# A Perceiver block with routed experts on one core: second-layer biases at the evacuation, first queries among the first scores, rotary tables as a step of their own, first expert weights sooner

## The chip, the core and the metric

The kernel runs on one core of a Trainium2 chip. The engines are TensorE (PE, its weight loads shown as PEld), VectorE (DVE), ScalarE (ACT), GpSimd (POOL) and SyncE (SP); each works through its own queue of instructions and waits on semaphores of the others. SP computes nothing here and issues most of the DMAs. All data are float32. The time is that of one execution on the device, in microseconds (us), and the median of several runs is compared. The kernel before took 834.33 us (median of 3 runs, 834.09 to 838.12).

## The reference

Input x has 64 sequences of 32 tokens with 256 channels (2048 tokens); each sequence has a context of 257 rows of 128 channels.

```python
x = x + xattn(layernorm(x), ctx)      # 16 heads of 64, no mask
x = x + attn(layernorm(x))            # 4 heads of 64, half of each head rotated by position
x = x + ffn(layernorm(x))

# attn: tables from one learned number
base = sigmoid(nrope_freq[0]) * SDT_L + MIN_L * BASE_FREQUENCY
inv_freq = base ** (-arange(16) / 16)
ang = pos[:, None] * inv_freq[None, :] * (2 * pi / (T - 1))     # cos(ang), sin(ang)

# ffn: 8 experts, 2 a token, gates renormalised over the two
scores = x @ Wr.T + br
h = x @ Wl1[n] + bl1[n]; a, b = split(h)
y[n] = (silu(a) * b) @ Wl2[n] + bl2[n]
out = sum over the two chosen n of gate[n] * y[n]
```

## The kernel before

Tokens are cut into 16 tiles of 128 (t = 0 to 15), each four sequences (b = 0 to 3). The program has three stages: a start, an attention loop over the 64 sequences, and an expert stage.

The queues of PE and SP keep the order in which the program is written; a planner orders the instructions of DVE, ACT and POOL, within their dependencies, before the program is compiled.

**Start.** `load` (L98) puts a DMA on SP's queue: the rotary base number `base` (L129), the first two tiles of x, the query weights `xwq_sb` and `xwk_sb` (1 MB and 0.5 MB, one DMA each, L132 and L133), the first context, then the other weights. POOL fills constants: `diag`, `u_ring` and `p_last` (L166 on) with zeros, and a row of iotas. `cross_queries(0)` (L305) normalises two tiles of x (`normed`: statistics on DVE, the inverse root as a power on POOL, the product on DVE), transposes them on PE, copies them on ACT to `xqT`, and makes the queries of 16 heads in four groups: `pqh` (PE, L345), its copy `qh` (ACT), `pq` (PE, L324, folding the key weights into the query), and its copy `q` by halves on DVE (L337) and ACT (L335). The rotary tables `cos` and `sin` are computed next in the text (L890 to L928): a sigmoid on ACT, a power of 16 elements on POOL (L913), two sines on ACT (L919, L920), doubled twice on DVE. After that the rest of `cross_queries(0)`, and `cross_probs` of the first sequence.

**Attention loop** (L935). For each sequence: `tp` transposes its probabilities (PE, L392), `s` makes scores of the next sequence in four groups (PE, L369), each with its negative maximum `nmx` (DVE, L373), exponential (ACT, L374), reciprocal of the sums and product `pr` (DVE, L379, L381), and `pa` mixes the context (PE, L402). Between these `step()` advances one of three generators by a unit, as the table `steps` (L875) says: six places for each of eight sequences, two tiles. "ahead" makes queries of the tiles to come. "near" is `rest` of the tile just finished and "far" that of the tile before it; `rest` runs `cross_output` (`pov`, `po`), `self_attention` (`trs`, `pqkv`, the rotation on DVE, `trqk`, `pss`, `pot`, `apo`) and `route` (L526). `route` ends with the expert choice (`trr`, `pr`), the slots (`pk`, L567, L568), two indirect DMAs by POOL which scatter the token rows and their gates into the DRAM table `routed` (L578), and the bias path: the eight gates of a token are transposed (`pw`, PE, L586), copied (DVE, L588), multiplied with the eight second-layer biases `b2` (`pb`, PE, L591), added to x (DVE, L592), and x is written to `out` (L595).

PSUM tiles called `bank` share three banks, in turn.

**Expert stage.** A block is 128 rows of `routed` of one expert. Six early blocks are formed from the tiles counted so far when t = 15 begins (`early_blocks`, L771), and 33 late ones at most after the last tile (`late_blocks`, L800, a long chain on DVE from the counts `pc_late` to the addresses `meta_late`). A block has the units x (`prepared`: rows transposed, gate and target row taken), a and b (first layer, by halves), c (`combined`: second layer `py`, its product with the gate by DVE, L762, and an indirect DMA of POOL that adds the rows to `out`, L763). Weights lie in three lanes of SBUF, the first layer in one tile (`wall1`) and the second in another (`wall2`, 4 KB a partition); a load is skipped when the expert stays the same. The end of the attention work and the early blocks are woven by a list of units written by hand (L1015 to L1025).

The early rows are fetched in the last tile (L974 to L977):

```python
        if t == NT - 1 and b == 2:
            load_last(t)
            for i in range(EARLY):
                blocks.gathered(i)
            blocks.weights(0, (0, 1), sure=True)
```

The tile `xg` that a gather fills has five buffers, and `EARLY` is 6.

Of the kernel before, what the change touches and what calls it, by code (L numbers as in the profile page):

```python
# [16 lines left out]
P = 128  # L17
# [18 lines left out]
W2LEN = 4 * D  # L36
# [14 lines left out]
def block_kernel(  # L51
# [21 lines left out]
    b2: bass.AP,  # L73
# [17 lines left out]
    half_pi = const.tile([P, 1], FP, name="half_pi")  # L91
    nc.gpsimd.memset(half_pi, math.pi / 2)
# [36 lines left out]
    load(base, freq.partition_broadcast(P))  # L129
    for t in range(2):  # L130
        load_tokens(t)
    load(xwq_sb, xwq.rearrange("(c p) k -> p c k", p=P))  # L132
    load(xwk_sb, xwk_t.rearrange("(c p) k -> p c k", p=P))  # L133
# [15 lines left out]
    b2_sb = const.tile([NE, D], FP, name="b2_sb")  # L149
# [7 lines left out]
    load(b2_sb, b2)  # L157
# [6 lines left out]

    diag = [const.tile([P, AH, P], FP, name=f"diag{i}") for i in range(2)]
    for d in diag:  # L166
        nc.gpsimd.memset(d, 0.0)

    u_ring = [const.tile([P, D], FP, name=f"u{i}") for i in range(3)]
    p_last = [
        [const.tile([P, 32], FP, name=f"p_last{i}_{b}") for b in range(4)] for i in range(2)
    ]
    for u in u_ring:
        nc.gpsimd.memset(u, 0.0)
    for ring in p_last:
        for p in ring:
            nc.gpsimd.memset(p, 0.0)

    def iota(shape, pattern, base, by_partition, name):
        it = const.tile([P] + shape, FP, name=name)
        nc.gpsimd.iota(
            it,
            pattern,
            base=base,
            channel_multiplier=by_partition,
            allow_small_or_imprecise_dtypes=True,
        )
        return it  # L190

    ones = const.tile([P, P], FP, name="ones")
    nc.gpsimd.memset(ones, 1.0)

    before = iota([P], [[1, P]], 0, -1, "before")
    nc.vector.tensor_scalar(before, before, 0.0, None, ALU.is_gt)
    region = iota([1, NE], [[0, 1], [CAP, NE]], 0, 0, "region")
    expert_id2 = iota([2, NE], [[0, 2], [1, NE]], 0, 0, "expert_id2")

    upto = iota([NE, NE], [[1, NE], [-1, NE]], 0, 0, "upto")  # L200
    nc.vector.tensor_scalar(upto, upto, 0.0, None, ALU.is_ge)

    late = iota([LATE], [[1, LATE]], 0, 0, "late")
    in_lane = iota([LATE // LANES, LANES], [[1, LATE // LANES], [0, LANES]], FAR, 0, "in_lane")
    late_expert = iota([LATE, NE], [[0, LATE], [1, NE]], 0, 0, "late_expert")

    early = iota([EARLY // 2, 2], [[1, EARLY // 2], [EARLY // 2, 2]], 0, 0, "early")
    early_expert = iota([EARLY, NE], [[0, EARLY], [1, NE]], 0, 0, "early_expert")
    row = iota([1], [[0, 1]], 0, 1, "row")
    minus_spare = iota([1], [[0, 1]], -TOK, -1, "minus_spare")  # L210
    token = iota([NT], [[P, NT]], 0, 1, "token")

    seen = const.tile([P, NE], FP, name="seen")
    nc.gpsimd.memset(seen, 0.0)
    xp = pool("xp", 3)
    none = xp.tile([P, RW], FP, tag="xg", bufs=5, name="none")
    nc.gpsimd.memset(none, 0.0)

    for e in range(NE):
        load(routed[e * CAP : e * CAP + P, :], none)  # L220

    load(out[TOK : TOK + P, :], none[:, :D])

# [4 lines left out]
    sm = pool("sm", 4)  # L228
    tb = pool("tb", 1)
# [4 lines left out]
    def normed(t, name, xn=None):  # L234
        st = sm.tile([P, 6], FP, tag="st", name=f"st{name}{t}")
        mv = sm.tile([P, 2], FP, tag="mv", name=f"mv{name}{t}")
        nc.vector.bn_stats(st, xs[t])
# [67 lines left out]
    def cross_queries(c):  # L305

        xqT = wk.tile([P, 2, 2 * P], FP, tag="xqT", name=f"xqT{c}")
        xns = [normed(2 * c + j, "q") for j in range(2)]
# [133 lines left out]
    def self_attention(t, xn):  # L442
# [4 lines left out]
        for lo, hi in ((0, 512), (512, 768)):  # L447
            pq = bank([hi - lo], f"pqkv{t}_{lo}")
            for k in range(2):
                nc.tensor.matmul(  # L450
                    pq, xaT[:, k, :], awqkv_sb[:, k, lo:hi], start=(k == 0), stop=(k == 1)
                )
            nc.vector.tensor_tensor(qkv[:, lo:hi], pq, abqkv_bc[:, lo:hi], ALU.add)

# [5 lines left out]
        nc.vector.tensor_tensor(x1s, x1, sb, ALU.mult)  # L460
# [64 lines left out]

    def route(t, xr):  # L526

# [56 lines left out]
        yield  # L584
        pw = bank([P], f"pw{t}")
        nc.tensor.transpose(pw[:NE, :], ew, ident)  # L586
        ewT = sm.tile([NE, P], FP, tag="rewT", bufs=2, name=f"rewT{t}")
        nc.vector.tensor_copy(ewT, pw[:NE, :])  # L588
        yield
        pb = bank([D], f"pb{t}")  # L590
        nc.tensor.matmul(pb, ewT, b2_sb, start=True, stop=True)  # L591
        nc.vector.tensor_tensor(xs[t], pb, xs[t], ALU.add)  # L592

        queue = nc.sync if t < NT - 2 else nc.gpsimd
        queue.dma_start(out=out[t * P : (t + 1) * P, :], in_=xs[t])  # L595
# [67 lines left out]
    class Blocks:  # L663
# [88 lines left out]
        def combined(self, b):  # L752
# [9 lines left out]
            nc.vector.tensor_scalar(y, py, self.gate[:, b : b + 1], None, ALU.mult)  # L762
# [37 lines left out]
    def late_blocks(done):  # L800
# [69 lines left out]


# [7 lines left out]
        ("near", "far", "ahead", "", "far", "far"),  # L879
# [3 lines left out]
        ("", "far", "near", "", "far", "far"),  # L883
# [5 lines left out]

    with tc.tile_pool(name="rope", bufs=1) as rp:  # L890
        pos = rp.tile([P, 1], FP, name="pos")
        for s in range(P // SEQ):
            nc.gpsimd.iota(
                pos[s * SEQ : (s + 1) * SEQ, :],
                [[0, 1]],
# [236 lines left out]
```

## Time and profile before

| what | value |
|---|---|
| median of 3 runs | 834.33 us (834.09 to 838.12) |
| the profiled execution | 835.06 us, span 833.3 us |
| mean granted PE clock | 0.994 |
| PE busy, 0 to 40 us | 25.4 of 40 us |
| PE busy, 100 to 600 us | 491.0 of 500 us |
| PE busy, 600 to 700 us | 94.0 of 100 us |
| pw and pb on PE | 4.4 and 11.1 us, 16 and 32 records |
| x<-pb,x on DVE (L592) | 16 times 424 ns |
| y_late on DVE (L762) | 28 times 484 ns |
| DMA moved | 62.71 MB, mean 75 GB/s |

The span is the stretch of the profiled execution in which the engines work; its own time is 1.8 us longer. An engine's busy time sums its instructions. A line of the timeline gives the start, the length, the engine, the line of the program, the operation, what is written from what is read, and how many instructions are merged; a bracket at the end gives how long the engine had been idle before and what ended that. A matrix product of float32 makes two records. Since PE overlaps successive records, the price of a group is read from its start to the start of the next.

### The profile page before, as it was taken

Reading aid. Unit: us, or ns where it says so; the run is one execution under the profiler, and the core shown is the slowest. Engines: PE = TensorE matmul, PEld = TensorE weight load, DVE = VectorE, ACT = ScalarE, POOL = GpSimd, SP = SyncE. Lnnn points to the kernel's source line nnn. Section 1 sums busy time; section 2 is a strip of 40 time slices with the busy share of each in tenths; the row PEclk is TensorE's granted clock in tenths of the full one; section 3 lists DMA queues with packets and bytes.
Section 4 is the critical chain, followed back from the end, with each engine's and each line's share of the span. In section 5 each row is a group of like instructions: output and inputs, shape, how many; then the busy total and the mean of one; then the engine's idle time right before and its main releaser. Section 6 shows DMA issues by size and latency. Waiting matters only on the chain. (4 is left out here: it accounts for less than half of the span.)

```text
span 833.3 us, 15141 instructions
## 1 busy us (share of the span) xinstructions
PE 792.6 (95%) x5240; PEld 613.0 (74%) x5240; DVE 490.1 (59%) x2006; ACT 378.5 (45%) x1080; POOL 147.2 (18%) x209
## 2 busy tenths in 40 slices
PE   4899999999999999999999999999988999999995
PEld 3577677767767676766777677666667899999994
DVE  2556756766676766667666766768646733333331
ACT  2565545545465555455554545455423322222221
POOL 5001011211111010112101010110112322332332
PEclk9999999999999999999999999999999999999998
DMA  8421102020211202020210202020162296348331
GB/s 304 130 55 54 64 1 74 1 87 8 67 41 46 74 1 87 1 75 19 68 45 30 74 1 74 7 68 26 35 237 43 64 356 182 57 101 232 52 47 21
DMA packets 32031, 62.71 MB, mean 75 GB/s; under 512 B 5256, under 2 KB 22672, under 8 KB 30416
## 3 DMA queue, kind: packets, MB, share of 16 engines
q1 hardware_dynamic: 25424, 52.65, 19.0%
q0 software_dynamic: 6528, 9.06, 6.2%
q8 instruction: 43, 0.70, 0.4%
q14 instruction: 36, 0.29, 0.1%
HBM read 83.23 MB, written 13.16 MB: 116 GB/s over the span
## 5 line engine op out<-in xcount | busy, mean ns | idle before, releaser
L374 ACT ACTIVATE pr<-s,nmx 128x257 f32<-128x257 f32 x256 | 120.8, 478 | 95.0 <-DVE nmx L373 93.0
L369 PE MATMUL s<-kv,q 128*128 128x257 f32 x512 | 141.3, 385 | 1.8 <-ACT pr L374 1.8
L373 DVE TENSOR_REDUCE nmx<-s 128x1 f32<-128x257 f32 x256 | 104.6, 421 | 63.5 <-PE s L369 62.1
L402 PE MATMUL pa<-pt,kv 128*128 128x512 f32 x256 | 123.4, 604 | 5.1 <-ACT ov L426 5.1
L369 PEld LDWEIGHTS s<-kv,q 128*128 128x128 f32 x512 | 88.3, 191 | 15.9 <-ACT pr L374 3.2
L396 ACT COPY pt<-tp 128x512 f32<-128x512 f32 x128 | 75.7, 592 | 38.9 <-PE tp L392 38.8
L392 PEld LDWEIGHTS tp<-ident,pr 128*128 128x128 f32 x512 | 60.7, 143 | 36.1 <-issue 21.1
L392 PE MATMUL tp<-ident,pr 128*128 128x128 f32 x512 | 82.7, 279 | 2.0 <-DVE pr L381 2.0
L381 DVE TENSOR_SCALAR pr<-pr,inv 128x256 f32<-128x256 f32 x256 | 79.9, 355 | 2.9
L405 ACT COPY cT<-pa 128x512 f32<-128x512 f32 x64 | 37.4, 584 | 87.5 <-PE pa L402 87.5
L402 PEld LDWEIGHTS pa<-pt,kv 128*128 128x128 f32 x256 | 45.0, 190 | 40.9 <-issue 29.9
L578 POOL DMA_INDIRECT routed<-xr,rslots x32 | 32.5, 1016 | 223.2 <-DVE rewT L588 80.6
L345 PE MATMUL pqh<-xqT,xwq_sb 128*128 128x256 f32 x256 | 62.8, 390 | 4.3 <-ACT xqT L253 4.3
L763 POOL DMA_INDIRECT out_x<-y_late,to_late x28 | 43.4, 1549 | 103.9 <-DMA out_x<-y_late,to_late 37.2
L435 PE MATMUL po<-xwo_sb,ov 128*128 128x256 f32 x256 | 60.6, 379 | 0.0
L345 PEld LDWEIGHTS pqh<-xqT,xwq_sb 128*128 128x128 f32 x256 | 48.8, 196 | 11.7 <-ACT xqT L253 4.7
L435 PEld LDWEIGHTS po<-xwo_sb,ov 128*128 128x128 f32 x256 | 48.6, 190 | 6.6
L410 POOL TENSOR_TENSOR xb<-x,xbo_bc 128x256 f32<-128x256 f32 x16 | 11.6, 725 | 236.8 <-issue 221.2
L379 DVE RECIPROCAL inv<-sums 128x2 f32<-128x2 f32 x128 | 20.6, 161 | 53.9 <-ACT pr L374 53.5
L374 ACT ACTIVATION_READ_ACCUMULATOR pr<-s,nmx 128x1 f32 x256 | 51.7, 202 | 0.0
L762 DVE TENSOR_SCALAR y_late<-py_late,gate_late 128x256 f32<-128x256 f32 x28 | 13.6, 484 | 62.0 <-PE py_late L757 62.0
L450 PE MATMUL pqkv<-awqkv_sb,xaT 128*128 128x512 f32 (+1 forms) x128 | 43.9, 486 | 0.0
(256 smaller groups left out, 1293.9 us busy)
## 6 DMA issues: line engine op xcount, KB each, us to landing
lane<-in_wall SPq DMA_DIRECT2D x24, 1028.0 KB
lane<-in_wall SPq DMA_DIRECT2D x24, 512.0 KB
lane2a<-in_wall SPq DMA_DIRECT2D x10, 1028.0 KB
kv<-in_ctx_t SPq DMA_DIRECT2D x16, 514.0 KB
kv<-in_ctx_a SPq DMA_DIRECT2D x16, 512.0 KB
lane2b<-in_wall SPq DMA_DIRECT2D x10, 512.0 KB
xg_late<-routed SPq DMA_DIRECT2D x28, 132.5 KB
x<-in_x SPq DMA_DIRECT2D x16, 128.0 KB
```

The lines of the kernel that those rows point to most:

```text
L345: nc.tensor.matmul(pq[:, mm, :], xwq_sb[:, k, m * P : (m + 1) * P], xqT[:, k, :], start=(k == 0), stop=(k == 1),)
L369: nc.tensor.matmul(s, qb[:, g * P : (g + 1) * P], kvT[:, b, :], start=True, stop=True)
L373: nc.vector.tensor_reduce(nmx, s, AX.X, ALU.max, negate=True)
L374: nc.scalar.activation(pr[:, g, :], s, AF.Exp, bias=nmx, accum_out=sums[:, g : g + 1])
L381: nc.vector.tensor_scalar(pr[:, i, :ML], pr[:, i, :ML], inv[:, i : i + 1], None, ALU.mult)
L392: nc.tensor.transpose(tp[:, g * P : (g + 1) * P], pr[:, g, j * P : (j + 1) * P], ident)
L396: nc.scalar.copy(pt, tp)
L402: nc.tensor.matmul(pa, kvA[:, b, j, :], pts[j], start=(j == 0), stop=(j == MC - 1))
L405: nc.scalar.copy(cT[:, :, b, :], pa.rearrange("p (h n) -> p h n", n=SEQ))
L435: nc.tensor.matmul(po, ov[:, m, :], xwo_sb[:, m, :], start=False, stop=(m == XH // 2 - 1))
L450: nc.tensor.matmul(pq, xaT[:, k, :], awqkv_sb[:, k, lo:hi], start=(k == 0), stop=(k == 1))
L763: nc.gpsimd.indirect_dma_start(out=out[:, :], out_offset=bass.IndirectOffsetOnAxis(ap=self.to[:, b : b + 1], axis=0), in_=y, in_offset=Non ...
```

## The change

There are five parts.

1. The second-layer bias no longer goes through `pw` and `pb`. `wall2` holds it as a fifth row of 256 columns, repeated over the partitions, so a lane's second tile has 5 KB a partition; `combined` adds it from there to `py` and multiplies by the gate after that. `route` ends with the scatter, and x is written to `out` at the end of `self_attention`.
2. The loads of `xwq` and `xwk` come in four pieces each. Ten products of the identity with itself open PE's queue. The scores of the first sequence are interleaved with its queries. The second pair of tiles gets its queries from the second sequence on.
3. The rotary tables are a function called at n = 5, with `base` loaded at n = 3; power series instead of sines, and an exponential instead of the sigmoid. The rotation in `self_attention` is a unit of its own, and its first instruction, like a few others, keeps its place in the program's order on its engine. Two of the eight rows of `steps` change, the fourth and the eighth.
4. The zeros of `diag`, `u_ring` and `p_last` are set by DVE, and the iotas stand after the first queries' normalisation.
5. The first early block's weights and five early rows are fetched after b = 1 of the last tile, weights first. The hand-written list changes, and lane 2's second tile takes a buffer of `cT` instead of one of `pr`.

```diff
-W2LEN = 4 * D
+W2LEN = 5 * D
...
-    load(base, freq.partition_broadcast(P))
     for t in range(2):
         load_tokens(t)
-    load(xwq_sb, xwq.rearrange("(c p) k -> p c k", p=P))
-    load(xwk_sb, xwk_t.rearrange("(c p) k -> p c k", p=P))
+    for i in range(4):
+        w = slice(4 * HD * i, 4 * HD * (i + 1))
+        load(xwq_sb[:, :, w], xwq[:, w].rearrange("(c p) k -> p c k", p=P))
+        load(xwk_sb[:, 2 * i : 2 * i + 2, :], xwk_t[w, :].rearrange("(c p) k -> p c k", p=P))
...
             nc.vector.tensor_tensor(qkv[:, lo:hi], pq, abqkv_bc[:, lo:hi], ALU.add)
+        yield
...
-        nc.vector.tensor_tensor(x1s, x1, sb, ALU.mult)
+        tc.keep_in_program_order(nc.vector.tensor_tensor(x1s, x1, sb, ALU.mult))
...
         nc.vector.tensor_tensor(xs[t], po, xb, ALU.add)
+        queue = nc.sync if t < NT - 2 else nc.gpsimd
+        queue.dma_start(out=out[t * P : (t + 1) * P, :], in_=xs[t])
...
-        yield
-        pw = bank([P], f"pw{t}")
-        nc.tensor.transpose(pw[:NE, :], ew, ident)
-        ewT = sm.tile([NE, P], FP, tag="rewT", bufs=2, name=f"rewT{t}")
-        nc.vector.tensor_copy(ewT, pw[:NE, :])
-        yield
-        pb = bank([D], f"pb{t}")
-        nc.tensor.matmul(pb, ewT, b2_sb, start=True, stop=True)
-        nc.vector.tensor_tensor(xs[t], pb, xs[t], ALU.add)
-
-        queue = nc.sync if t < NT - 2 else nc.gpsimd
-        queue.dma_start(out=out[t * P : (t + 1) * P, :], in_=xs[t])
...
-            nc.vector.tensor_scalar(y, py, self.gate[:, b : b + 1], None, ALU.mult)
+            nc.vector.tensor_tensor(y, py, w[:, 4 * D :], ALU.add)
+            nc.vector.tensor_scalar(y, y, self.gate[:, b : b + 1], None, ALU.mult)
...
+    def rotary_tables():
...
+            tc.keep_in_program_order(
+                nc.scalar.activation(sig, base, AF.Exp, bias=zero, scale=-1.0)
+            )
+            tc.keep_in_program_order(nc.vector.tensor_scalar(sig, sig, 1.0, None, ALU.add))
+            nc.vector.reciprocal(sig, sig)
...
+            nc.gpsimd.tensor_tensor(root[0], base2, part, ALU.pow)
...
+            for i in range(4):
+                n = 1 << i
+                nc.vector.tensor_scalar(
+                    inv_freq[:, n : 2 * n], inv_freq[:, 0:n], root[i], None, ALU.mult
+                )
...
+            def series(acc, highest):
+                nc.vector.tensor_scalar(acc, sq, term(highest), None, ALU.mult)
+                for n in range(highest - 2, 1, -2):
+                    nc.vector.scalar_tensor_tensor(acc, acc, term(n), sq, ALU.add, ALU.mult)
...
-        ("near", "far", "ahead", "", "far", "far"),
+        ("near", "", "ahead", "near", "", "far"),
...
-        ("", "far", "near", "", "far", "far"),
+        ("", "", "near", "near", "", "far"),
...
+    for d in diag:
+        nc.vector.memset(d, 0.0)
...
+    warm = bank([P], "warm")
+    for _ in range(10):
+        nc.tensor.matmul(warm, ident, ident, start=True, stop=True)
+    scores = cross_probs(0, 0, kvs[0][0])
+    for i in range(5):
+        next(work["ahead"])
+    next(scores)
+    for i in range(2):
+        next(work["ahead"])
+    next(scores)
     for _ in work["ahead"]:
         pass
-    work["ahead"] = cross_queries(1)
-    next(work["ahead"])
-    for _ in cross_probs(0, 0, kvs[0][0]):
+    for _ in scores:
         pass
     for n, (t, b) in enumerate(seqs):
+        if n == 1:
+            work["ahead"] = cross_queries(1)
+            next(work["ahead"])
+        if n == 2:
+            next(work["ahead"])
+        if n == 3:
+            load(base, freq.partition_broadcast(P))
+        if n == 5:
+            rotary_tables()
...
-        if t == NT - 1 and b == 2:
+        if t == NT - 1 and b == 1:
             load_last(t)
-            for i in range(EARLY):
+            blocks.weights(0, (0, 1), sure=True)
+            for i in range(EARLY - 1):
                 blocks.gathered(i)
-            blocks.weights(0, (0, 1), sure=True)
...
-    lane2 = pp.tile([P, 4, M], FP, tag="pr", name="lane2b").rearrange("p g m -> p (g m)")
+    lane2 = wk.tile([P, XH, 4, SEQ], FP, tag="cT", name="lane2b")
...
-    do("near far near a0 far x1 b0 near far near c0 near a1 near far b1 x2 far a2 near c1")
-    do("far near x3 b2 far near c2 far near a3 near x4 b3")
+    do("far near near a0 far x1 b0 near far near near c0 near a1 near far b1 x2 far a2 near c1")
+    do("far near x3 b2 a3 near c2 near x4 b3 near a4")
     late, total = late_blocks(done)
-    do("a4 c3")
+    do("c3")
...
-    do("near b4 near x5 a5 c4")
+    do("b4 x5 a5 c4")
...
-        "wall2": by_row("Wl2", 4),
-        "b2": a["L0_ffn_bl2"],
+        "wall2": np.concatenate(
+            [by_row("Wl2", 4), np.repeat(a["L0_ffn_bl2"], P, axis=0)], axis=1
+        ),
```

## The prediction, made before the changed kernel ran

> **What bounds the kernel now.** I read the page first, then a table of the busy time by stage, then the order of instructions at the places where TensorE (PE) sat idle or slow. The page's busy time by engine says where to look:
>
> ```profile
> PE 792.6 (95%) x5240; PEld 613.0 (74%) x5240; DVE 490.1 (59%) x2006; ACT 378.5 (45%) x1080; POOL 147.2 (18%) x209
> ```
>
> PE is busy for 792.6 of 833.3 us, so about 41 us are gaps, and everything else must come from PE work itself. The table by stage (length, then busy time and instructions of each engine, clock, DMA share, GB/s) shows where the gaps lie:
>
> ```profile
> 0.00:10.00 10.00, 1.22 (x4) 0.58 (x4) 2.84 (x13) 2.86 (x3) 9.07 (x48) 1.00 0.72 238
> 10.00:20.00 10.00, 7.23 (x26) 5.54 (x27) 2.15 (x12) 2.47 (x7) 1.38 (x2) 1.00 0.99 371
> ...
> 300.00:400.00 100.00, 98.56 (x648) 70.35 (x646) 70.53 (x290) 54.26 (x155) 15.50 (x25) 1.00 0.14 45
> ...
> 600.00:650.00 50.00, 44.91 (x343) 35.12 (x342) 26.54 (x120) 16.97 (x38) 11.30 (x12) 0.97 0.35 120
> ...
> 750.00:790.00 40.00, 40.00 (x308) 38.56 (x308) 14.23 (x62) 10.81 (x36) 10.85 (x7) 1.00 0.58 144
> ```
>
> The attention loop (98.56 of 100) and the expert stage (40.00 of 40) have no gap to speak of: there, time falls only with PE work. Gaps are in the first 35 us and around 600 to 665. The start, all engines in order of time:
>
> ```profile
> 8.46 2.91 POOL L913 TENSOR_TENSOR inv_freq<-base,expo 128x16 f32<-128x16 f32 x1
> ...
> 11.68 0.31 ACT L919 ACTIVATE s<-ang,zero 128x16 f32<-128x16 f32 x1 [5.40 <-DVE ang L915]
> ...
> 12.09 0.62 ACT L253 COPY xqT<-trq 128x256 f32<-128x256 f32 x2
> ...
> 12.77 5.85 PE L345 MATMUL pqh<-xqT,xwq_sb 128*128 128x256 f32 x16 [4.28 <-ACT xqT L253]
> ```
>
> The first transposes end at 8.5 us, but their copy sits on ACT behind the two sines, which wait for POOL's power. And the first 16 query records take 5.85 us, 366 ns each, where later groups of 8 take 1.99: PE is slow at first. The bias path in the PE order:
>
> ```profile
> 604.91 0.27 PE L586 MATMUL pw<-ident,xr 128*8 128x128 f32 x1
> 605.09 1.95 PE L402 MATMUL pa<-pt,kv 128*128 128x512 f32 x4
> 606.97 0.69 PE L591 MATMUL pb<-b_sb,rewT 8*128 8x256 f32 x2
> 607.72 1.97 PE L418 MATMUL pov<-cT,xwv_sb 128*64 128x128 f32 x32
> ```
>
> Since records overlap, the price is start to next start: 0.18 and 0.75 us here; elsewhere 0.10 and 0.11 for pw, 0.62 and 0.63 (three times) for pb. Last the first expert weights, on SP's queue, on POOL and on PE:
>
> ```profile
> 582.48 28.38 SPq L680 DMA_DIRECT2D xg_early<-routed  x6
> 611.43 0.87 SPq L689 DMA_DIRECT2D lane<-in_wall  x2
> ```
>
> ```profile
> 613.30 1.06 POOL L578 DMA_INDIRECT routed<-xr,rslots  x1 [17.00 <-DMA xg_early<-routed]
> ```
>
> ```profile
> 616.95 2.98 PE L726 MATMUL pa_early<-bxT_early,lane 128*128 128x128 f32 x16 [1.92 <-DMA lane<-in_wall]
> ```
>
> Six gathers into five buffers: the sixth waits until x0 on PE has read the first, so weights issued behind it start at 611 and land at 617, and POOL's scatter, which must follow the gathers, holds POOL for 17 us.
>
> **What the Trainium skill says.** "TensorE: Matmul & The Clock Gate", section "Part 1: The HAM clock gate": PE runs at half clock until some 3.4 us of sustained work. The trace agrees in kind: 366 against about 240 ns a record. The same section calls ACT and DVE strict FIFO; the copy behind the sines is that. "ScalarE: Activation LUTs", section "What ACT_TABLE_LOAD costs": 1283 ns and a drain for each change of set; the trace shows 1.28 us, three times before the first exponential. "DMA: Bandwidth & Descriptors", section "Specifications": line rate needs 512 B or more, so quarter loads of xwq (1 KB rows) keep it; no run here shows that pattern yet.
>
> **The change part by part**, against the profiled execution, 835.06 us (span 833.3 and 1.8 around it).
>
> Start. No sine, no base load ahead of x (0.45 us on SP), and POOL's memsets and iotas stand behind the first two powers in the order of after. The x tiles landed at 3.66 us, so now about 3.2; statistics and power (0.43, 0.18, 0.15, then POOL 0.55 each), normalising (0.41 each) and transposes bring the copies to 6.0 and 6.6, the first query matmul to about 7.05 instead of 12.77. The memsets now on DVE (two of 128x512, three of 128x256, eight small) cost 0.52, 0.27 and 0.07 each on POOL, 2.4 us in all, ahead of x's landing; bounds 0 to 1 us if DVE is slower. Ten warm-up matmuls run from 1.6 us in a gap and should have the clock up: the 16 records then take 3.5. Loads: at the rates of before (GB/s in two-microsecond stretches, summed: 0.94 MB by 6 us, 1.62 by 8, 2.38 by 10) the first quarter of xwq and xwk (0.65 MB with x) is there by 5.1, all four by 8.7, ctx_t by 10; even a third slower none is late. From 7.05: query matmuls 1.75 a piece, pq 1.06, scores 0.44, with evacuations of 0.6 on ACT and 0.7 on DVE. The one stall that I find is PSUM: the fourth pq needs the bank that DVE empties after the first pair's normalisation, some 1.7 us. Second-sequence scores then start at 24.7 instead of 33.58: **-8.9** (bounds -6 to -10.5).
>
> Bias in the attention loop. 13 of the 16 tiles' pw and pb stand there: 13 x (0.12 + 0.64) = **-9.9**. DVE loses 0.27 + 0.42 a tile. What is late next: the fourth row of each tile, where pb filled PE between the last scores and the next transposes. The softmax chain from the end of the last scores takes 2.0 us there (scores end 130.1, last pr at 132.08). After, PE has pa 1.75 and pk 0.43, since pk was moved there: 2.2. Just covered. I add **+1** for rows that aren't (0 to +5).
>
> Rotary tables. Some 37 DVE instructions of 0.17 us and one POOL power that DVE waits for, 0.9: 7.3 us, at t=1, b=1, in order with the softmax. DVE was 11.97 of 20 busy at 60 to 80, so 3.6 us free in a sequence of 9: **+2.5** (0 to +5). The rotation in each tile gets its own unit, no new work: of its six instructions one (0.28) stands between the last maximum and the reciprocal.
>
> Early weights and the new unit list. Between 596 and 667 PE waits 1.10, 1.92, 0.67, 0.42, 0.49, 1.40, 0.52 and 0.36 = 6.9, and pa_early and pot run 1.03 and 0.46 slow. Weights now go out a sequence and more earlier, ahead of five gathers that wait for no buffer: the 1.92, the slow 1.5, and POOL's 17 us with the waits for its powers (1.10, 0.67, 1.40) should go. SP's queue behind them holds only lane loads. Three tiles' bias also: 2.3. New: from pc_late to the first late gather landed takes 11.5 us (653.4 to 664.9), a DVE chain of 40; PE had 12.4 us of work before it needs it. With a4 ahead of pc_late (1.87) and pw and pb gone (0.74) it has 9.8; 1.7 are missing, 0.2 of DVE work leaves the chain: **+1.5** (0 to +3). With 1.5 for the other short waits, 8.4 + 2.3 - 3.0 = **-7.7** (-4 to -9).
>
> Evacuation. Each of 34 blocks trades 0.484 (tensor_scalar from PSUM) for 0.424 (as x<-pb,x) and about 0.35 (as pr<-pr,inv): +0.3 on DVE, a third busy in that stage, hidden by PE. The last block's chain is open:
>
> ```profile
> 823.59 0.48 DVE L762 TENSOR_SCALAR y_late<-py_late,gate_late 128x256 f32<-128x256 f32 x1 [1.31 <-PE py_late L757]
> 824.53 1.55 POOL L763 DMA_INDIRECT out_x<-y_late,to_late  x1 [2.90 <-DVE y_late L762]
> ```
>
> **+0.35**. Second-layer loads grow from 512 to 640 KB, 0.35 us each at 370 GB/s. From 666 to 698 the queues are full (350 to 402 GB/s): 1.54 MB in 5.5 us a block becomes 1.67, still below; **+0.3** (0 to +4).
>
> Sum: -8.9 - 9.9 + 1 + 2.5 - 7.7 + 0.35 + 0.3 = -22.4; 812.7 in the profiled execution, and 0.7 less by the median (834.33): **812.0**.
>
> **Rivals.** (a) The loop turns to waiting for the softmax: without pb as filler, half of the 9.9 comes back, and the tables cost 5: 812 + 5 + 2.5 = 819.5. For it: at 94.97, in a fourth row with no routing to fill it, PE waited 0.83 for pr. Against: PE waited for pr three times in all, 2.0 us. (b) More is gained: tables and rows hide (-3.5), the late gather is in time (-1.5): 807. For it: DVE is 59% busy. (c) The expert stage becomes bound by weights: each of some ten full loads +0.35 and a late issue, +4: 816; against it, PE had no wait there. (d) **Slower**: the pinned rotation. Its first instruction is held in program order, and if the two bias adds and six rotations (0.69 + 0.42 + 6 x 0.28 = 2.8 us) stood between the last maximum and the reciprocals, each of 16 tiles would pay 2.8: +45, against 22.4 gained, 857. It decides from 1.4 us a tile. Against it: in the order of after one instruction stands there.
>
> **How the numbers follow.** Forecast 0.55 (808 to 817 alone), (a) 0.20, (b) 0.13, (c) 0.08, (d) 0.04. 806 to 822 takes in the forecast, (a), (c) and most of (b): 8 in 10. A change below 0.5%, 4 us, can't be told from none here; only (d) and a failure of several parts together come near: faster 0.94, same 0.02, slower 0.04.
>
> **What would show it.** Right: the first query matmul near 7 us at about 220 ns a record, second-sequence scores near 25, no wait for lane at the first pa_early, POOL's scatter without its 17 us, and PE at 98 to 99 of 100 in the loop. A PE wait of 1 to 2 us at the first pxT_late, and one near t=1, b=1. Wrong: waits for pr in each fourth row, or lane waits from 660 on.

## The result, and the profile after

The changed kernel took 810.17 us (median of 4 runs, 808.9 to 811.86) against 835.75 us of the kernel before beside it: a ratio of 0.9693, 95% interval 0.9658 to 0.9729. A later set of five gave 809.88 us and 0.9671 (0.9653 to 0.9689). Predicted were 812.0 us, within 806 to 822. The profiled span fell from 833.3 to 809.3 us, 24.0 against the 22.4 of the sum. The sum came out well partly because errors cancelled: the start was put 2.9 us too high, and the loop (bias, uncovered rows and rotary tables together) 5.8 us too low. So this section splits the 24 us first.

The page's busy time by engine, and the table by stage with the stretches of before (length, busy time and instructions of PE, PEld, DVE, ACT, POOL, then granted clock, DMA share, GB/s):

```profile
PE 778.6 (96%) x5212; PEld 612.5 (76%) x5212; DVE 496.9 (61%) x2045; ACT 378.3 (47%) x1078; POOL 143.7 (18%) x195
```

```profile
20.00:30.00 10.00, 8.23 (x39) 6.30 (x40) 6.00 (x18) 4.93 (x15) 0.39 (x1) 0.83 0.77 215
300.00:400.00 100.00, 98.68 (x652) 73.10 (x651) 69.16 (x276) 53.54 (x154) 15.09 (x23) 1.00 0.16 52
600.00:650.00 50.00, 45.48 (x355) 40.69 (x354) 31.56 (x155) 20.11 (x47) 15.92 (x15) 1.00 0.31 84
750.00:790.00 40.00, 40.00 (x305) 38.45 (x304) 15.94 (x65) 10.91 (x37) 12.42 (x8) 1.00 0.31 48
```

PE has 14 us less work and 10 us less of gaps. Loop and expert stage are as full as before (98.68 of 100, 40.00 of 40): what the loop gained, it gained in PE's busy time without a new gap. The stretch from 600 to 650 us, in the transition between loop and expert stage, still has 4.5 us of gaps. New is a clock of 0.83 between 20 and 30 us.

Compare the start of the same record in both traces, and the gain in us can be read off along the way:

| mark | before | after | gain so far | gain of the stage | predicted |
|---|---|---|---|---|---|
| second-sequence scores | 33.58 | 24.77 | 8.8 | 8.8 | 8.9 |
| first `po` of tile 0 | 69.98 | 63.97 | 6.0 | -2.8 | 0 |
| `po` of tile 1 | 103.4 | 97.6 | 5.9 | -0.2 | -2.5 (tables) |
| `po` of tile 13 | 551.1 | 532.8 | 18.3 | 12.4 | 8.9 |
| first `pa_late` | 666.82 | 642.35 | 24.5 | 6.2 | 7.7 |
| end of the span | 833.3 | 809.3 | 24.0 | -0.5 | -0.65 |

From `po` of tile 1 to that of tile 13 stand the bias paths of 12 tiles; the prediction's term had 13, so here the thirteenth counts with the transition.

**Start.** The order of PE's instructions (start, length, engine, line, operation, tiles, shapes, count, and the idle time before with what ended it), and the clock in two stretches:

```profile
7.46 3.80 PE L285 MATMUL pqh<-xqT,xwq_sb 128*128 128x256 f32 x16 [0.46 <-ACT xqT L192]
...
24.35 0.62 PE L332 MATMUL tp<-ident,pr 128*128 128x128 f32 x2 [1.57 <-DVE pr L321]
24.77 1.93 PE L309 MATMUL s<-kv,q 128*128 128x257 f32 x4
```

```profile
24.00:26.00 2.00, 1.65 (x5) 1.34 (x6) 0.88 (x5) 0.58 (x1) 0.00 (x0) 0.68 0.84 278
26.00:28.00 2.00, 2.00 (x8) 1.65 (x7) 0.72 (x2) 1.38 (x5) 0.00 (x0) 0.50 0.86 174
```

Queries begin 5.3 us sooner and run at 238 ns a record. Then PE idles 1.57 us for the first softmax, and four scores that took 1.03 us before take 1.93: the granted clock is 0.50 for about 3.4 us, from 24.7 to 28.1. By the first `po`, 2.8 of the 8.8 us are gone.

**Loop.** The fourth row of `steps` (and the eighth, which is the fourth of the next tile) is where the bias path stood. In every second of these rows PE also makes `qkv`. Such a row in PE's order, first before, then after:

```profile
166.33 0.60 PE L369 MATMUL s<-kv,q 128*128 128x257 f32 x2
166.76 0.27 PE L586 MATMUL pw<-ident,xr 128*8 128x128 f32 x1
166.87 1.88 PE L402 MATMUL pa<-pt,kv 128*128 128x512 f32 x4
168.69 0.69 PE L591 MATMUL pb<-b_sb,rewT 8*128 8x256 f32 x2
169.31 0.95 PE L392 MATMUL tp<-ident,pr 128*128 128x128 f32 x4
170.09 1.03 PE L369 MATMUL s<-kv,q 128*128 128x257 f32 x4
```

```profile
159.62 1.88 PE L342 MATMUL pa<-pt,kv 128*128 128x512 f32 x4
161.33 0.28 PE L510 MATMUL pk<-rboth,before 128*128 128x8 f32 x2
161.47 0.37 PE L511 MATMUL pk<-seen,ones 128*128 128x8 f32 x2
161.70 0.64 PE L332 MATMUL tp<-ident,pr 128*128 128x128 f32 x4
162.17 0.60 PE L309 MATMUL s<-kv,q 128*128 128x257 f32 x2
```

From start to next start, before: `pw` 0.11, `pa` 1.82, `pb` 0.62, `tp` 0.78. After: `pa` 1.71, `tp` 0.47. Besides `pw` and `pb` themselves, `pa` lost 0.1, and `tp` lost a stall of 0.31 that the trace did not show as a wait. A tile gains 0.88 us where the fourth row has no `qkv` and 1.18 where it has, 1.03 in the mean; the prediction had 0.76 less 1 us in all.

**Transition.** Three of PE's waits there, and POOL's order around the last of them:

```profile
611.62 2.05 PE L657 MATMUL pa_early<-bxT_early,lane 128*128 128x128 f32 x16 [0.50 <-ACT bxT_early L631]
...
623.68 0.41 PE L191 MATMUL trr<-ident,xr 128*128 128x128 f32 x2 [1.43 <-DVE xr L184]
...
642.10 0.41 PE L629 MATMUL pxT_late<-ident,xg_late 128*128 128x128 f32 x2 [0.59 <-DMA xg_late<-routed]
```

```profile
588.78 1.06 POOL L521 DMA_INDIRECT routed<-xr,rslots  x1 [11.75 <-DVE gate_early L636]
...
621.86 0.61 POOL L468 DMA_DIRECT2D out_x<-x  x1 [1.51 <-DMA out_x<-y_early,to_early]
622.49 0.60 POOL L181 TENSOR_TENSOR rstdr<-ver,minus_half 128x1 f32<-128x1 f32 x1
```

No wait for the lane is left, and the scatter no longer waits 17 us for the gathers. But the last `trr` waits 1.43 us as before (1.40), now because POOL's power stands behind the write of the tile, which waits 1.51 us for an accumulating DMA.

**Last block.** Two evacuating instructions in the place of one, as priced:

```profile
799.12 0.42 DVE L693 TENSOR_TENSOR y_late<-py_late,lane2b 128x256 f32<-128x256 f32 x1 [1.31 <-PE py_late L688]
799.58 0.35 DVE L694 TENSOR_SCALAR y_late<-y_late,gate_late 128x256 f32<-128x256 f32 x1
```

### The profile page after: what moved, and what is told of

The parts are those of the page before. It is cut to its first block, busy times and chain, and to the rows that moved or that the text cites. A ratio compares the mean times of both kernels' runs of the same rounds, so it can differ in the third digit from the quotient of the medians.

```text
span 809.3 us, 15134 instructions
## 1 busy us (share of the span) xinstructions
PE 778.6 (96%) x5212; PEld 612.5 (76%) x5212; DVE 496.9 (61%) x2045; ACT 378.3 (47%) x1078; POOL 143.7 (18%) x195
## 5 line engine op out<-in xcount | busy, mean ns | idle before, releaser
L321 DVE TENSOR_SCALAR pr<-pr,inv 128x256 f32<-128x256 f32 x256 | 82.3, 363 | 3.3
L332 PE MATMUL tp<-ident,pr 128*128 128x128 f32 x512 | 80.2, 278 | 1.6 <-DVE pr L321 1.6
L285 PE MATMUL pqh<-xqT,xwq_sb 128*128 128x256 f32 x256 | 60.8, 381 | 0.8 <-ACT xqT L192 0.8
L631 ACT COPY bxT_late<-pxT_late 128x256 f32<-128x256 f32 x28 | 10.4, 372 | 73.1 <-PE pxT_late L629 73.1
```

Of the source, the lines that this page charges most:

```text
L285: nc.tensor.matmul(pq[:, mm, :], xwq_sb[:, k, m * P : (m + 1) * P], xqT[:, k, :], start=(k == 0), stop=(k == 1),)
L321: nc.vector.tensor_scalar(pr[:, i, :ML], pr[:, i, :ML], inv[:, i : i + 1], None, ALU.mult)
L332: nc.tensor.transpose(tp[:, g * P : (g + 1) * P], pr[:, g, j * P : (j + 1) * P], ident)
```

## The experiments

All times are medians. The kernel before took 834.78 to 836.85 us beside them, and a ratio is to the kernel before of the same set. Where a part is small, I read it in the trace, from mark to mark: the start of the kernel before, which e1, e3, e5 and e9 share, differs between these executions by up to 2.4 us at the first `po`. Its first 16 query records took 5.49 to 6.78 us (the clock column reads 1.00 there too), and in e3 and e5 the clock fell to 0.50 once more, near 32 us.

| run | time | ratio to before (95%) | span |
|---|---|---|---|
| bias alone (e1) | 829.93 | 0.9938 (0.9916 to 0.9960) | 827.2 |
| start alone (e2) | 827.77 | 0.9911 (0.9885 to 0.9937) | 826.3 |
| early weights alone (e3) | 832.13 | 0.9951 (0.9935 to 0.9967) | 830.9 |
| changed, rotation in qkv's unit (e4) | 817.27 | 0.9786 (0.9762 to 0.9809) | 815.4 |
| rotation alone (e5) | 830.16 | 0.9939 (0.9921 to 0.9957) | 830.8 |
| changed, pk first (e6) | 811.17 | 0.9716 (0.9698 to 0.9733) | 809.8 |
| changed, pv in the gap (e7) | 808.55 | 0.9689 (0.9668 to 0.9710) | 806.8 |
| changed, write after the power (e8) | 809.13 | 0.9694 (0.9676 to 0.9713) | 806.2 |
| the loop's whole change (e9) | 819.22 | 0.9820 (0.9788 to 0.9852) | 815.8 |
| changed, no warm-up (e10) | 810.26 | 0.9703 (0.9678 to 0.9728) | 808.0 |
| three repairs (e11) | 804.61 | 0.9633 (0.9605 to 0.9661) | 803.5 |
| changed again (e12) | 809.88 | 0.9671 (0.9653 to 0.9689) | 808.7 |

### Why does the loop gain more than the bias path costs? (e1, e4, e5, e6, e9)

**e1**, the kernel before with the bias at the evacuation. `pk` stays at the head of the fourth row and the rotation in the unit of `qkv`:

```diff
-        ("near", "far", "ahead", "", "far", "far"),
+        ("near", "far", "ahead", "", "", ""),
...
-        ("", "far", "near", "", "far", "far"),
+        ("", "far", "near", "", "", ""),
...
-        pw = bank([P], f"pw{t}")
...
-        nc.vector.tensor_tensor(xs[t], pb, xs[t], ALU.add)
...
+            nc.vector.tensor_tensor(y, py, w[:, 4 * D :], ALU.add)
```

> The kernel before with the second-layer bias moved to the evacuation and nothing else: pw and pb are gone, their two places in the fourth row of each tile are empty, pk stays at the row's beginning, the rotation stays in the unit of qkv. Theory 1 (the rotation decides): in every second fourth row six rotation instructions, 1.1 us on DVE, still stand between the last score maximum and its evacuation, so there PE meets a wait for pr of about 0.8 us and gains only some 0.35 a tile, while the other fourth rows gain 0.84. Loop from tile 0 to tile 13: -7.5 us; with the transition's -2.3 and the last evacuation's +0.4 the time is 9 to 10 below before. Rival, the prediction's step (pw and pb are priced alone, 0.76 a tile wherever they stand, the fourth rows just covered): loop -9.9 us, no wait for pr, 12 below before. Rival 2 (the 1.03 a tile seen in the changed kernel belongs to the bias alone): loop -13, 15 below.

It gained 2.9 us from tile 0 to tile 12 and 5.5 in all (835.41 to 829.93). The row with `qkv`, PE's order and then DVE's:

```profile
167.38 0.38 PE L389 MATMUL tp<-ident,pr 128*128 128x128 f32 x2
168.60 0.56 PE L389 MATMUL tp<-ident,pr 128*128 128x128 f32 x2 [0.84 <-DVE pr L378]
```

```profile
165.30 0.29 DVE L457 TENSOR_TENSOR x1s<-qkv,sin 128x128 f32<-128x128 f32 x1
...
166.64 0.29 DVE L462 TENSOR_TENSOR qkv<-qkv,x1s 128x128 f32<-128x128 f32 x1
166.84 0.42 DVE L370 TENSOR_REDUCE nmx<-s 128x1 f32<-128x257 f32 x1
...
168.10 0.62 DVE L378 TENSOR_SCALAR pr<-pr,inv 128x256 f32<-128x256 f32 x2
```

All six rotation instructions stand between the first evacuation of `qkv` and the row's last maximum (166.84), so the last `pr` comes at 168.7, and PE, which has only `pa` left as cover (work that it can do meanwhile), waits. The 0.84 us that `pw`, `pb` and `pa` lost come back in `tp` (0.78 to 1.62): a tile gains 0.00 there. In the other rows it gains 0.67 once and 0.45 later, since `tp` there grows from 0.49 to 0.65 and then 0.87. I had expected 0.35 and 0.84: the direction was right, the stall too small. That the price is gained wherever it stands is refuted: alone, the bias brings less than a third of the 9.9 us in the loop. The prediction had counted `pk` behind `pa` as cover; e1 lacks it there, e4 has it.

**e4**, the changed kernel with the rotation back in the unit of `qkv`:

```diff
             nc.vector.tensor_tensor(qkv[:, lo:hi], pq, abqkv_bc[:, lo:hi], ALU.add)
-        yield
...
-        tc.keep_in_program_order(nc.vector.tensor_tensor(x1s, x1, sb, ALU.mult))
+        nc.vector.tensor_tensor(x1s, x1, sb, ALU.mult)
...
-        ("near", "", "ahead", "near", "", "far"),
+        ("near", "", "ahead", "", "", "far"),
...
-        ("", "", "near", "near", "", "far"),
+        ("", "", "near", "", "", "far"),
```

> The changed kernel with the rotation put back into the unit of qkv, no instruction of it held in order; the rest as changed. Theory: in every second fourth row the last score maximum waits on DVE behind six rotation instructions, about 1 us, and without pb as cover PE waits for pr some 0.75 us there: seven tiles, +5 to +6 us in the loop, the other rows unchanged, 5 to 6 above the changed kernel (about 815.5). Rival, the prediction's step (a unit of its own moves no work and costs or brings nothing): the same time as the changed kernel within 1 us.

It is 7.1 us slower than the changed kernel (817.27 against 810.17). From tile 1 to tile 13, the step in each row with `qkv` is +1.10 and in each other row 0.00; six rows make 6.6. The row of e4 shows it:

```profile
161.99 0.56 PE L332 MATMUL tp<-ident,pr 128*128 128x128 f32 x2 [0.75 <-DVE pr L321]
```

Set the changed kernel's DVE beside it. One rotation instruction stands ahead of the maximum and one behind, and the rest follow `pr`:

```profile
159.25 0.29 DVE L402 TENSOR_TENSOR x2s<-qkv,sin 128x128 f32<-128x128 f32 x1
159.46 0.41 DVE L393 TENSOR_TENSOR qkv<-pqkv,abqkv_bc 128x256 f32<-128x256 f32 x1
159.82 0.42 DVE L313 TENSOR_REDUCE nmx<-s 128x1 f32<-128x257 f32 x1
160.16 0.28 DVE L404 TENSOR_TENSOR qkv<-qkv,cos 128x128 f32<-128x128 f32 x1
...
161.07 0.62 DVE L321 TENSOR_SCALAR pr<-pr,inv 128x256 f32<-128x256 f32 x2
...
161.68 0.29 DVE L401 TENSOR_TENSOR x1s<-qkv,sin 128x128 f32<-128x128 f32 x1
```

In e4 all six stand ahead of it, which makes the maximum 0.98 us later against the evacuation of `qkv`, and `pr` another 0.3, since there three instructions of `pk` have also slipped in ahead of the reciprocal (161.00 to 161.29). So not all of the 1.10 is the rotation's own.

**e5**, the kernel before with this edit alone (the lines of e4's diff the other way round, `far` units kept). Neither e4 nor e5 separates the new unit from the instruction held in its place.

> The kernel before with the rotation as a unit of its own, first instruction held in order, and nothing else; the bias path stays. Theory (the same queue on DVE, but with pb as PE's cover): in every second fourth row the last maximum comes about 0.9 us sooner, PE's stall of 0.31 us in the transposes behind pb goes, the other rows stay: 7 x 0.31, about 2 us below before, so that rotation and bias together bring more (13) than each alone (2 and 3). Rival, the prediction's step (a unit of its own moves no work): the same time as before within 1 us. Rival 2 (the rotation is worth the 7 us that the fourth experiment showed, with the bias or without): 7 below.

The trace gives 0.30 a row with `qkv` and 0.00 in the others, 1.8 us from tile 1 to tile 13; the row from tile 0 to tile 1, which has no `pb`, gains 0.97. The span is 2.5 below that of before, the median 4.6 (834.78 to 830.16). `tp` behind `pb` takes 0.49 there instead of 0.78. So the stall of before was this queue on DVE, and its size depends on what PE has as cover: 0.31 behind `pb`, 0.97 to 1.10 without it.

**e6**, the changed kernel with `pk` at the head of the row:

```diff
-        ("near", "", "ahead", "near", "", "far"),
+        ("near", "far", "ahead", "near", "", ""),
...
-        ("", "", "near", "near", "", "far"),
+        ("", "far", "near", "near", "", ""),
```

> The changed kernel with the two pk records of each tile back at the beginning of the fourth row, so that only pa (1.72 us) lies between the last scores and the next transposes. The prediction's step: the softmax chain takes 2.0 us, pa and pk together 2.2, so without pk PE waits about 0.25 us in each of 13 rows: +3 us. Theory from the changed trace: in the rows with qkv the evacuation ends level with PE and some 0.3 us more shows, in the others 0.2: +2 to +4. Rival (DVE is free enough there, the place of pk is worth nothing): within 1 us of the changed kernel.

It lost 0.20 to 0.22 us in each row of both kinds, 2.5 us from tile 1 to tile 13. The place of `pk` was rightly priced. At the end of the span only 0.5 are left of it, since this execution was 1.4 ahead at the first `po`, having kept its clock (below), and 0.6 come back in the transition. The median rose by 1.0 (811.17).

**e9**, the kernel before with all three: bias, rotation, `pk`.

> The kernel before with the loop's whole change: bias at the evacuation, rotation a unit of its own, pk behind pa in the fourth row; start and early weights as before. Theory (the parts depend on each other): alone, the bias took 2.9 us from tile 0 to tile 12 and the rotation 1.8; together both kinds of fourth row are free of waits and the loop loses 12 us there, the whole time falls by some 15, to 820. Rival (the parts add): 2.9 + 1.8 = 4.7 us in the loop, the time near 825.

It gained 12.2 us from tile 0 to tile 12, and 15.9 in all (835.07 to 819.22). Alone, bias and rotation gave 2.9 and 2.5 over the same stretch (the 1.8 of the expectation leaves out the first row). So the parts do not add: 12.2 against 5.4. The steps are 0.88 and 1.18, those of the changed kernel. The first one, from tile 0 to tile 1, where no bias path ran yet, is 0.97 as in e5. That row is one which the prediction had in its hands, in the kernel before:

```profile
94.97 0.56 PE L392 MATMUL tp<-ident,pr 128*128 128x128 f32 x2 [0.83 <-DVE pr L381]
```

It is the only row of the loop with `qkv` that has no `pb`, and it shows what all of them would look like with the bias gone and the rotation left: e1's wait is 0.84.

### The transition (e3, e8)

**e3**, the kernel before with the first weights at b == 1, ahead of five gathers:

```diff
-        if t == NT - 1 and b == 2:
+        if t == NT - 1 and b == 1:
             load_last(t)
-            for i in range(EARLY):
+            blocks.weights(0, (0, 1), sure=True)
+            for i in range(EARLY - 1):
                 blocks.gathered(i)
-            blocks.weights(0, (0, 1), sure=True)
```

> The kernel before with the first expert weights issued a sequence earlier and ahead of five gathers, and nothing else. Theory (the lane wait was the only loss there): PE's wait of 1.92 us for the lane at the first pa_early and the half clock behind it, 1.5 us, go; the waits for the last normalised rows (trr, 1.10 and 1.40 us) stay, since POOL gets there late for other reasons: 3.4 us below before. Rival, the prediction's step: with POOL's 17 us the waits of 1.10, 0.67 and 1.40 go as well: 6.5 below. Rival 2: the weights load now collides with something earlier and half comes back: under 2 below.

It gained 3.3 us (835.41 to 832.13). From `po` of tile 13 to the last `trr` it gains 4.9, of which 1.3 return by the end of the span. The lane's wait, the slow clock behind it and the 0.67 at `trs` are gone, and the last `trr` waits 0.57 instead of 1.40:

```profile
641.81 0.44 PE L252 MATMUL trr<-ident,xr 128*128 128x128 f32 x2 [0.57 <-DVE xr L245]
```

Between theory and rival: POOL's hold did cost part of those waits. In the changed kernel this part was lost again, as **e8** shows, the changed kernel with the write of a tile one unit later (behind the transposes of `route`):

```diff
-        queue = nc.sync if t < NT - 2 else nc.gpsimd
-        queue.dma_start(out=out[t * P : (t + 1) * P, :], in_=xs[t])
...
         transposed(xT, xr, 2, f"r{t}")
         yield
+        queue = nc.sync if t < NT - 2 else nc.gpsimd
+        queue.dma_start(out=out[t * P : (t + 1) * P, :], in_=xs[t])
```

> The changed kernel with the write of a finished tile issued one unit later, so that on POOL the power of tile 15's last normalisation no longer stands behind a DMA that waits for an accumulating one. Theory (that order, not the scatter of before, holds the last trr): PE's wait of 1.43 us for xr at 624 us goes and 1.4 us stay gained to the end. Rival (the gathers of the late blocks set the end of the transition): the wait moves to the first pxT_late, 0.82 us there becomes about 2, and nothing is gained.

The last `trr` has no wait any more, 1.6 us less there; but the `trr` of tile 13 waits 1.71 instead of 0.80, which gives 0.9 back. For this one I have no cause; e11, which moves the last tile's write alone, does not have it. The start, where this execution is 2.0 ahead, set apart, 1.1 us remain in the span. The write ahead of the power was what held the last `trr`; the late gather did not take its place (one wait of 0.67, for 0.82 in two).

### The start (e2, e7, e10, e12)

**e2**, the kernel before with the start alone (split loads, memsets, warm-up, interleaving, tables at n == 5).

> The kernel before with the start alone changed: loads split, memsets on DVE, warm-up, first queries interleaved with scores, rotary tables at the second tile; bias, rotation unit and early weights as before. Theory: the second sequence's scores start near 24.8 us (33.58 before), then PE waits 1.57 us for pr, the granted clock falls to half for 3.3 us, and by the first po the gain is 6.0; nothing of it changes later: 6 us below before in all. Rival (the tables cost 2.5 us between tile 0 and tile 1 because DVE is busier in a kernel that still has the bias adds): 3.5 below before, with PE waits for pr of 2 us or more between 60 and 80 us.

It is 7.6 us below before by the first `po`, 6.5 from `po` of tile 1 on, 7.6 in the median (827.77). Between the two, the tables cost 1.1: on DVE the maxima of the scores queue among their instructions, and PE waits 1.0 us once. The surprise: the same gap of 1.58 us for the first softmax is there, and the clock stayed at 1.00 behind it.

**e7**, the changed kernel with `pv` moved into the gap:

```diff
     for _ in scores:
         pass
+    next(work["near"])
     for n, (t, b) in enumerate(seqs):
...
-            if name:
+            if name and not (n == 0 and name == "near"):
```

> The changed kernel with the 16 pv records (1.73 us of work that is due anyway) moved from the first row to before the first transposes, where PE waits 1.57 us for the first softmax. Theory: that wait is filled, and the half clock that followed it in the profile of the changed kernel, 2 us, can't come; against it pa and the next transposes lose pv as cover, about 0.6. 1 us below the changed kernel where that had kept its clock, 3 us below its profiled execution, in the start to the first po. Rival (the softmax chain of the second sequence sets the pace and all is given back): no difference by the first po.

It took 808.55 us. Measured against e8, which has the same start and kept its clock, the first `po` comes only 0.1 us sooner: my 1 us is refuted, and the rival is right. The 1.67 us by which e7's PE is ahead of e8's near 30 us end at one record; e8's line first, then e7's:

```profile
34.02 0.70 PE L309 MATMUL s<-kv,q 128*128 128x257 f32 x2 [0.41 <-ACT pr L314]
```

```profile
33.90 0.70 PE L309 MATMUL s<-kv,q 128*128 128x257 f32 x2 [1.95 <-ACT pr L314]
```

DVE of e7 in that time, ahead of the maxima of the third sequence:

```profile
30.02 0.41 DVE L184 TENSOR_SCALAR xnq<-x,mvq,rstdq 128x256 f32<-128x256 f32 x1 [0.66 <-POOL rstdq L181]
...
31.84 0.41 DVE L184 TENSOR_SCALAR xnq<-x,mvq,rstdq 128x256 f32<-128x256 f32 x1 [0.66 <-POOL rstdq L181]
32.17 0.68 DVE L225 COPY u_all<-pu 128x512 f32<-128x512 f32 x1
32.77 1.08 DVE L313 TENSOR_REDUCE nmx<-s 128x1 f32<-128x257 f32 x3
```

Twice DVE waits for POOL's power of the second pair of tiles, whose first statistics are held in program order, and the maxima queue behind.

**e10**, the changed kernel without its ten warm-up matmuls.

> The changed kernel without the ten warm-up matmuls on PE. The prediction's step: with a cold start the first 16 query records take 5.85 us as before instead of 3.8, and their beginning at 7.4 us stays: 2 us above the changed kernel by the first scores. Rival (the transposes and the gap-free start bring the clock up in time, or later waits hide it): under 0.5 us.

The 16 query records took 5.69 us instead of 3.80, as expected, but began at 6.80 instead of 7.46, so 1.1 us were lost at the transposes behind the 1.58 us gap; there the clock then held, and at the first `po` this execution is 0.5 ahead of the changed kernel's. The times (810.26 and 810.17) can't be told apart.

**e12**, the changed kernel unaltered, once more.

> The changed kernel once more, unaltered, for another profiled execution. In its first profile PE idled 1.57 us at 24 us and then had half the clock for about 3.3 us, which cost 2.0 us; three kernels with the same gap of 1.58 us at the same place kept the clock. Theory (the drop depends on when the gap falls, not on the kernel): this profile may show a clock of 1.00 from 24 to 28 us, and then stands 2.0 us below the first one from the first po to the last record, 807.3 us in span. Rival (the drop belongs to this kernel): half clock at the same place, and 809.3 us again.

The hoped-for case did not come. The half clock is there again at the same place, and the first `po` comes within 0.05 us of that in the first profile:

```profile
24.00:26.00 2.00, 1.70 (x6) 1.34 (x7) 0.94 (x5) 0.58 (x1) 0.00 (x0) 0.68 0.80 266
26.00:28.00 2.00, 2.00 (x8) 1.70 (x7) 0.61 (x2) 1.49 (x5) 0.00 (x0) 0.50 0.83 207
```

So the changed kernel had it in both of its profiles, and e2, e4, e6, e8 and e10 did not, with a gap of 1.58 us that ended between 23.9 and 25.4 us. But this does not refute the theory. In all six profiles with such a fall ahead of the end of the span (before, changed, e2, e3, e5, e12) the half clock lasts 3.41 us, and from there to the fall at the end lie 61, 228 or 232 times 3.41 us: the clock changes on a grid of steps of 3.41 us. Laid back to the gap, that grid shows how busy PE was in the steps around it:

| profile | PE busy in the steps around the gap, us of 3.41 | clock after |
|---|---|---|
| changed, e12 | 1.84 and 1.83, one step each | 0.50 |
| e4 | 2.12, then 2.99 | 1.00 |
| e6 | 2.19, then 2.43 | 1.00 |
| e2 | 2.37, then 2.39 | 1.00 |
| e8 | 2.42, then 2.70 | 1.00 |
| e10 | 2.68, then 2.48 | 1.00 |

In both profiles of the changed kernel the gap lies within one step (21.3 to 24.7 us), in the other five it lies across two steps, neither of them below 2.12. So e12 happened to repeat the position of the first profile and could not decide. Four of the nine runs of the changed kernel had spans of 806.9 to 807.5 us, where the theory has 807.3 with the clock kept; they have no profile, so whether they kept it is not shown.

### A faster version (e11)

**e11** has `pv` in the gap, the statistics of both tiles of the second pair ahead of both products, and only the last tile's write behind its power:

```diff
+        if c == 1:
+            parts = [statistics(2 * c + j, "q") for j in range(2)]
+            yield
+            xns = [scaled(2 * c + j, "q", *parts[j]) for j in range(2)]
+        else:
+            xns = [normed(2 * c + j, "q") for j in range(2)]
```

> The changed kernel with three repairs: pv before the first transposes; the statistics of both tiles of the second pair ahead of both normalisations, so that DVE doesn't wait twice for POOL's power in front of the third sequence's maxima; the last tile's write one unit later, so that POOL's power stands ahead of it. Theory: at the start the 1.95 us wait for pr that pv's move had left behind falls to under 0.7, 1.3 us below the seventh experiment by the first po; the last trr doesn't wait, 1.4 us less by the end of the transition of which 0.5 returns at the late gather: 806 us. Rival (the start is given back once more, to the next chain): 807.5, the last trr alone.

It took 804.61 us, 0.9633 of before. In its profile the wait of 1.95 us is gone, the first `po` stands 1.9 us below e7's (1.3 expected) and 4.05 below the changed kernel's, the last `trr` has no wait and gains 1.6, and the span is 803.5. It was not timed beside the changed kernel; over the kernel before, the intervals 0.9605 to 0.9661 and 0.9653 to 0.9689 (e12) overlap at the edge, so the profile carries the claim more than the times do.

## Why the prediction was right, and where it was not

The direction, the range and the main places were right; that the total was so near is luck, because errors cancelled.

- **Start, -8.9.** Right to 0.1 us at the mark that it named, by luck. The first query matmul came at 7.46 for 7.05. The PSUM stall of 1.7 did not come: two waits of 0.28 and 0.19 for `q` stand there. In its place PE waits 1.57 us for the `pr` of the first softmax, ahead of that mark, which the prediction left out. It was also wrong to end the sum at the mark: by the first `po` the gain is 6.0. Of the 2.8 lost, the half clock took some 1.6 (e8, which kept it, is 0.47 ahead at the mark and 2.03 at `po`), waits for `pr` and `xqT` 0.39 and 0.35; for the rest I have no cause.
- **Bias in the loop, -9.9, and +1 for rows not covered.** Measured -12.4 for 12 tiles. The price of `pw` and `pb` (0.73 a tile) held, and `pa` added 0.1. What failed is the step "The rotation in each tile gets its own unit, no new work". It moved five of six instructions from ahead of the last maximum to behind it. That is worth 0.3 us in each row with `qkv` while `pb` covers it, and 1.10 in the changed kernel (e5, e4). The softmax chain of 2.0 us was read in a row without `qkv`. In the row with `qkv` shown above the scores end at 166.9 and the last `pr` at 169.8, 2.9 us, more than the 2.2 of `pa` and `pk`:

```profile
167.94 0.42 DVE L373 TENSOR_REDUCE nmx<-s 128x1 f32<-128x257 f32 x1
...
169.19 0.62 DVE L381 TENSOR_SCALAR pr<-pr,inv 128x256 f32<-128x256 f32 x2
```

"Just covered" was right for the place of `pk` (0.25 a row worked out, 0.21 measured in e6), but it holds only with the rotation out of the way.
- **Rival (a)**, the loop waiting for the softmax, is what the bias change does alone (e1). The evidence named for it, 0.83 at 94.97, was the right one, and "PE waited for pr three times in all" no answer: the other rows had `pb` in that place.
- **Rival (b)**, more gained, was right for the rows, for another reason than the free DVE that it named; the tables (1.1) and the late gather (0.82) did not hide.
- **Rival (d)** had the right instructions and the wrong sign. One instruction stands between last maximum and reciprocal, as read from the order; the question to put was how many stood ahead of that maximum before.
- **Tables, +2.5.** Mis-sized: 1.1 (e2), one wait of 1.0 us near t = 1, b = 1, where it was expected. The prediction's own figures, 7.3 us of work less 3.6 free, would give 3.7; how 2.5 follows it does not say. In the table of marks only 0.2 show, since the rotation gains 0.97 in the same row (e4).
- **Transition, -7.7.** Measured -6.2. The lane wait, the slow clock and POOL's 17 us went as said (e3), the late gather costs 0.82 for 1.5. What failed is that POOL's late powers "should go" with them: the wait of 1.40 stayed at 1.43, because the write of the tile now stands ahead of the power on POOL (e8), and that of 1.10 stayed at 0.80. The prediction had counted the DMAs on SP's queue here, not this one on POOL's.
- **Evacuation and weights, +0.35 and +0.3.** 0.5 together. No wait for a lane in the expert stage: rival (c) is out for the changed kernel.

## What to carry to other kernels

When work leaves the busy engine, it also leaves as cover: look for the row that already lacks it, for its wait is what all rows will show. Of an instruction that is held in its place, ask on both sides what stood ahead of the waiting one before and after, and price it with the cover that will be left. A term for a stage ends where the next stage is as full as before, not at the first mark that moved.

## What the runs showed of the hardware

The Trainium skill ("TensorE: Matmul & The Clock Gate", section "Part 1: The HAM clock gate") has the clock fall after an idle window of about 3.4 us, a window that runs freely. In this case's traces it fell to 0.50 for 3.41 us, on a grid of 3.41 us, and the grid lay differently to the program from run to run (a step begins at 23.2 us in e8, at 23.6 in e6, at 24.7 in the changed kernel): that agrees with the free-running window. But PE was not idle for a whole window. The fall came behind single waits of 1.57 us (changed kernel) and 1.92 us (before, at the lane), and did not come behind 1.58 in five kernels, nor behind 1.96 at the first `pa_early` of e1, whose 16 records took 2.05 us where those of before took 2.98. Six steps in which PE was busy for 1.48 to 1.84 of 3.41 us had the fall behind them. Steps of 1.57 (e9), 1.64 (e5) and 1.70 (e8) in the transition had not, so busy time as the trace models it does not decide alone. What else does is open.
